# Windowed attention of layer 2: the values' shift folded into the output's, values and keys evicted by ScalarE, the output's shift added on GpSimd

## The chip, the core and the metric

The kernel is one program on one core of a Trainium2 chip. A core has five engines that run their own instruction queues side by side: TensorE (PE, with its weight loads shown as PEld), VectorE (DVE), ScalarE (ACT), GpSimd (POOL) and SyncE (SP, which here only issues transfers). The metric is the device time of one execution in microseconds; the median of five runs counts.

## What is computed

The network has four layers. Layers 0 and 1 are attentions over all tokens of a small image; layer 2 is an attention within windows of 64 tokens and then a mixture of experts; layer 3 is an additive attention and another mixture of experts. The change touches the windowed attention alone. Cut to what matters, it is:

```python
t = _to_tokens(x)                            # 2 images x 1024 tokens, 256 channels
# t = t + attention(_ln_t(t)):
x = jnp.roll(x, -shift, axis=1)              # windows shifted by half a window
qkv = xw @ w_qkv.T + b_qkv                   # 8 heads of 32
sim = jnp.einsum('bwphd,bwqhd->bhwpq', q, k) * scale + rel_pos[:, idx]
probs = jax.nn.softmax(sim, axis=-1)
out = jnp.einsum('bhwpq,bwqhd->bwphd', probs, v)
out = out @ w_out.T + b_out
```

The tokens `t` then go through a layer norm, a router and the experts.

## The kernel before

The 2048 tokens are 16 tiles (NT) of 128 tokens, 8 tiles (IT) for each image; a tile holds two windows of 64. All tokens stay in SBUF in one tensor `t`. `window_attention` first loads its weights and shifts, norms the first image and turns it to channels by partitions (`normed(0)`). Then it runs a loop of 20 slots, in which the steps of several tiles overlap:

- `value(i)`: the values of tile i, two matmuls into PSUM (`ps_va`), taken to SBUF (`va`) by VectorE, which adds the row `b_v` on the way (line 893 of the profile).
- `scores(i)`: 32 small matmuls (`ps_s`), then on VectorE scale and bias (`l`, L868), maximum (`wa_m`, L874), subtraction (L875); the exponential on ScalarE (L876); the sum (L877) and its inverse (`wa_rec`, L878) on VectorE; and on GpSimd the product with the inverse into one of three `probs` buffers (L881, two instructions).
- `turn(i - 2)`: eight transposes of `probs` on TensorE (`ps_pt`, L900), two evictions by ScalarE (`ptT`, L901).
- `project(g, part)`: while tiles are left, one quarter of the next group's queries (`qh`, evicted by ScalarE, L850) or keys (`kh`, evicted by VectorE, L852). A group is four tiles.
- `sums(i - 3)`: 16 small matmuls (`ps_av`), evicted by ScalarE (`oT`, L917).
- `output(i - 4)`: two matmuls (`ps_wo`), then VectorE adds the row `b_out` (`y`, L927) and GpSimd adds `y` to the tile of `t` (L928).

In the first six slots the loop also draws on `normed(1)`, the norm and the transposes of the second image (`ps_tr`, L832, evicted at L834). From slot 10 on it draws three steps a slot from `late.dispatch(2, 0)`, which routes the first image for the experts: the statistics of the tiles that are ready (`n_st`, L1079, which reads `t`), an inverse root (`ir_...`, L1064 to L1071), the normed tokens (`u`, L1089), their transposes (L1100), the router (L1129), the slots' numbers (`rt_...`), and 16 indirect transfers from GpSimd's queue that scatter the tokens to memory (`slots_in`, L1153). The experts read them back (`xr`, L1363), and their weights are fetched on GpSimd's queue too (`ew`, L1314).

All PSUM tiles of the loop but `ps_s` and `ps_av` come from one pool of three buffers (`late.misc`), so each new one waits until the third before it is evicted. The order of the instructions on TensorE and ScalarE is the program's (`tc.manual_schedule(engines={engines.PE, engines.Activation})`). On VectorE, GpSimd and SyncE a scheduler orders them by its own estimate of when each is ready. The order on every engine is fixed before the program runs, and each engine works strictly in it.

Of the kernel before, what the change touches and what calls it, by code (L numbers as in the profile page):

```python
# [19 lines left out]
F32 = mybir.dt.float32  # L20
I32 = mybir.dt.int32
U32 = mybir.dt.uint32
AF = mybir.ActivationFunctionType
ALU = mybir.AluOpType
# [3 lines left out]
P = 128  # L28
B, C, N = 2, 256, 1024
T = B * N  # L30
NT = T // P
CC = C // P
# [32 lines left out]
def broadcast(ap, shape):  # L65

    return ap.unsqueeze(len(shape) - 1).to_broadcast(shape)


class Stack:  # L70
# [699 lines left out]
    def window_attention(self, t, late):  # L770
# [5 lines left out]
        tc, nc = self.tc, self.nc  # L776
        H, D = 8, 32
        with ExitStack() as ctx:
            w = ctx.enter_context(tc.tile_pool(name="wa_w", bufs=1))
            sb = ctx.enter_context(tc.tile_pool(name="wa_sb", bufs=2))  # L780
# [4 lines left out]
            w_qkv = self.load(w, "w_qkv", "(c p) o -> p c o", p=P)  # L785
            w_out = self.load(w, "wa_w_out", "(c p) o -> p c o", p=P)
            b_qk = self.load(w, "b_qk")
            b_v, b_out = self.load_row(w, "b_v"), self.load_row(w, "wa_b_out")


            rel = self.ins["rel_pos"]
# [1 line left out]
            bias = w.tile([P, H, WIN], F32, name="bias")  # L793
# [18 lines left out]
                nc.gpsimd.memset(x, 0.0)  # L812

            uT, q, k, v, pT, o = {}, {}, {}, {}, {}, {}

            def normed(b):

                u = w.tile([P, IT, C], F32, name="u")
                uT[b] = w.tile([P, CC, N], F32, name=f"uT{b}")
                mv = self.mv[:, b * IT : (b + 1) * IT, :]  # L820
                rs = late.inverse_root(mv[:, :, 1], 1e-5)
                yield
                for i in range(IT):
                    nc.vector.tensor_scalar(
                        u[:, i, :], t[:, b * IT + i, :], mv[:, i, 0:1], rs[:, i : i + 1], ALU.subtract, ALU.mult
                    )
                yield
                for half in range(2):
                    for c in range(CC):
                        ps = late.misc([P, 4, P], "ps_tr")  # L830
                        for j in range(4):
                            nc.tensor.transpose(ps[:, j, :], u[:, 4 * half + j, c * P : (c + 1) * P], self.ident)  # L832
                        to = uT[b][:, c, half * CH : (half + 1) * CH].rearrange("p (k t) -> p k t", t=P)
                        (nc.scalar.copy if c else nc.vector.tensor_copy)(to, ps)  # L834
                        yield

            def project(g, part):

                if part == 0:
                    q[g], k[g] = (sb.tile([P, CC, CH], F32, name=n) for n in ("qh", "kh"))  # L840
                x, at = uT[g // 2], g % 2 * CH
                ps = late.misc([P, CH], "ps_qk")
                for c in range(CC):
                    nc.tensor.matmul(  # L844
                        ps, lhsT=w_qkv[:, c, part * P : (part + 1) * P], rhs=x[:, c, at : at + CH],
                        start=(c == 0), stop=(c == CC - 1),
                    )
                to = (q if part < CC else k)[g][:, part % CC, :]
                if part < CC:
                    nc.scalar.activation(to, ps, AF.Identity, bias=b_qk[:, part : part + 1])  # L850
                else:
                    nc.vector.tensor_scalar(to, ps, b_qk[:, part : part + 1], None, ALU.add)  # L852

            def scores(i):

                g, at = i // 4, (i % 4) * P
                s = p_s.tile([P, 4, CH], F32, name="ps_s")
                for o in range(CC):
                    for h in range(4):
                        rows = slice(D * h, D * (h + 1))  # L860
                        for r in range(2):
                            cols = slice(at + WIN * r, at + WIN * (r + 1))
                            nc.tensor.matmul(
                                s[WIN * r : WIN * (r + 1), h, WIN * o : WIN * (o + 1)],
                                lhsT=q[g][rows, o, cols], rhs=k[g][rows, o, cols], start=True, stop=True,
                            )
                l = sb.tile([P, H, WIN], F32, name="l", bufs=3)
                nc.vector.scalar_tensor_tensor(  # L868
                    l.rearrange("p (h o) k -> p h (o k)", o=CC), s[:, :, : CC * WIN], float(D) ** -0.5,
                    (last if (i + 1) % IT == 0 else bias).rearrange("p (h o) k -> p h (o k)", o=CC),  # L870
                    ALU.mult, ALU.add,
                )
                m, rec = (self.small.tile([P, H], F32, name=f"wa_{n}") for n in ("m", "rec"))
                nc.vector.tensor_reduce(m, l, AX.X, ALU.max)  # L874
                nc.vector.tensor_tensor(l, l, broadcast(m, [P, H, WIN]), ALU.subtract)  # L875
                nc.scalar.activation(l, l, AF.Exp)  # L876
                nc.vector.tensor_reduce(m, l, AX.X, ALU.add)  # L877
                nc.vector.reciprocal(rec, m)  # L878
                for r in range(2):
                    rows = slice(WIN * r, WIN * (r + 1))  # L880
                    nc.gpsimd.tensor_tensor(  # L881
                        probs[i % RING][rows, :, rows], l[rows], broadcast(rec[rows], [WIN, H, WIN]), ALU.mult
                    )

            def value(i):
                x = uT[i // IT][:, :, i % IT * P : (i % IT + 1) * P]
                v[i] = sb.tile([P, C], F32, name="va", bufs=4)
                ps = late.misc([P, C], "ps_va")
                for c in range(CC):
                    nc.tensor.matmul(  # L890
                        ps, lhsT=x[:, c, :], rhs=w_qkv[:, c, 2 * C :], start=(c == 0), stop=(c == CC - 1)
                    )
                nc.vector.tensor_tensor(v[i], ps, b_v, ALU.add)

            def turn(i):
                pT[i] = sb.tile([P, H, P], F32, name="ptT")
                for half in range(2):
                    ps = late.misc([P, H // 2, P], "ps_pt")
                    for h in range(H // 2):
                        nc.tensor.transpose(ps[:, h, :], probs[i % RING][:, H // 2 * half + h, :], self.ident)  # L900
                    nc.scalar.copy(pT[i][:, H // 2 * half : H // 2 * (half + 1)], ps)  # L901

            def sums(i):

                ps, x, y = p_av.tile([P, CC, P], F32, name="ps_av"), pT.pop(i), v.pop(i)
                for o in range(CC):
                    for h in range(4):
                        at = D * (4 * o + h)
                        nc.tensor.matmul(
                            ps[D * h : D * (h + 1), o, :], lhsT=y[:, at : at + D], rhs=x[:, CC * h + o, :],  # L910
                            start=True, stop=True,
                        )
                to_o(i, ps)
# [5 lines left out]
            def output(i):  # L919
                x = o.pop(i)  # L920
                ps = late.misc([P, C], "ps_wo")
                for c in range(CC):
                    nc.tensor.matmul(
                        ps, lhsT=x[:, c, :], rhs=w_out[:, c, :], start=(c == 0), stop=(c == CC - 1)
                    )
                y = sb.tile([P, C], F32, name="y")
                nc.vector.tensor_tensor(y, ps, b_out, ALU.add)  # L927
                nc.gpsimd.tensor_tensor(t[:, i, :], t[:, i, :], y, ALU.add)  # L928

            for _ in normed(0):  # L930
                pass
# [2 lines left out]
            with tc.manual_schedule(engines={engines.PE, engines.Activation}):  # L934
                for part in range(2 * CC):
                    project(0, part)
                for i in range(NT + 4):
                    if i < NT:
                        value(i)
                        scores(i)  # L940
                    if 2 <= i < NT + 2:
                        turn(i - 2)
                    if i + 4 < NT:
                        project(i // 4 + 1, i % 4)
                    if i < 6:
                        next(other, None)
                    if 3 <= i < NT + 3:
                        sums(i - 3)
                    if 4 <= i:
                        output(i - 4)  # L950
                    if i >= 10:
                        for _ in range(3):
                            next(route, None)
# [875 lines left out]
```

## Time and profile before

| | us |
|---|---|
| median of 5 runs | 2952.39 (2951.13 to 2954.48) |
| the profiled execution | 2956.82 |
| its span | 2955.1 |
| busy in the span: PE / DVE / ACT / POOL | 2719.4 / 1949.4 / 1828.7 / 1240.5 |
| the windowed attention: first norm to last scatter | about 1689 to 1868 |
| mean granted TensorE clock | 0.962 |

Times in the trace are counted from the span's start. The rows of a timeline are start, length, engine, line, operation, what is written and read, and in brackets how long the engine had been idle and who ended that. A row of the chain of waits is start, length and what held the end up at that moment. In a table by windows each engine's entry is its busy time and, in brackets, its instructions.

### The profile page before, as it was taken

To read this page: it belongs to the slowest core of one execution; us is meant where nothing else is said; L and a number is where in the kernel's file an instruction comes from. 1 tells how busy PE (TensorE), PEld (TensorE's weight loads), DVE (VectorE), ACT (ScalarE), POOL (GpSimd) and SP (SyncE) were. 2 spreads that over 40 slices of the span, in tenths; PEclk is the share of its full clock that TensorE was granted. 3 is DMA by queue.
4 is the path that set the end of the run, shared out by engine and by line. 5 is a ranking of instruction groups with operands and counts; after the bars stand their busy time and mean duration, and the time that the engine had idled before them with its cause. 6 is when DMAs were issued, how large, how long until landed. Compare 5 with 4: busy or idle time off the path is not lost. (4 is left out here: it accounts for less than half of the span.)

```text
span 2955.1 us, 77089 instructions
## 1 busy us (share of the span) xinstructions
PE 2719.4 (92%) x32006; PEld 1678.7 (57%) x32006; DVE 1949.4 (66%) x3642; ACT 1828.7 (62%) x2685; POOL 1240.5 (42%) x1302
## 2 busy tenths in 40 slices
PE   7899999999999999789999787899899989899987
PEld 3455555555555555555555445799666633355676
DVE  5899999999999999568778667543522343124242
ACT  2777777777777777345555322111499889788722
POOL 4777777777777777201111132443211021102142
PEclk9999999999999999899999897899999989899998
DMA  3000000000000000111110000443222010322354
GB/s 130 2 3 3 3 3 3 3 3 3 3 3 3 3 3 3 36 32 24 24 24 17 10 19 3 152 164 101 83 79 76 24 31 20 136 67 84 112 162 126
DMA packets 180574, 131.37 MB, mean 44 GB/s; under 512 B 130992, under 2 KB 162368, under 8 KB 173056
## 3 DMA queue, kind: packets, MB, share of 16 engines
q0 software_dynamic: 29232, 81.71, 8.3%
q1 hardware_dynamic: 149552, 44.27, 6.7%
q8 instruction: 251, 4.11, 0.6%
q10 hardware_dynamic: 1440, 0.47, 0.1%
q14 instruction: 99, 0.81, 0.1%
HBM read 181.24 MB, written 29.49 MB: 71 GB/s over the span
## 5 line engine op out<-in xcount | busy, mean ns | idle before, releaser
L143 PE MATMUL ps_s<-kT,qT 64*32 64x512 f32 x8192 | 605.9, 598 | 15.0 <-ACT sc L153 14.4
L200 DVE STREAM_TRANSPOSE wt<-sc 128x1024 f32<-128x1024 f32 x512 | 602.2, 1210 | 2.5 <-ACT sc L188 2.5
L188 ACT ACTIVATE sc<-sc,sa_shift 128x1024 f32<-128x1024 f32 x512 | 584.2, 1145 | 9.8 <-DMA sa_shift<-sa_min 9.5
L1614 ACT ACTIVATE th<-kT,qb 128x1024 f32<-128x1024 f32 x512 | 540.3, 1134 | 69.3 <-PE ps_e L1623 44.6
L210 PEld LDWEIGHTS ps_o<-wt,v 128*64 128x64 f32 x8192 | 446.4, 138 | 214.8 <-issue 206.8
L210 PE MATMUL ps_o<-wt,v 128*64 128x128 f32 x8192 | 506.3, 277 | 7.6 <-DVE oT L367 7.6
L153 ACT COPY sc<-ps_s 128x1024 f32<-128x1024 f32 x256 | 259.1, 1012 | 293.1 <-DVE sa_min L178 154.9
L166 POOL TENSOR_TENSOR fold<-sc 128x512 f32<-128x512 f32 x256 | 330.1, 1289 | 256.1 <-ACT sc L153 256.1
L168 POOL TENSOR_TENSOR fold<-sc,fold 128x512 f32<-128x512 f32 x256 | 328.1, 1282 | 21.4
L1623 PE MATMUL ps_e<-th,pick 128*32 128x512 f32 x2048 | 306.8, 620 | 22.1 <-ACT th L1614 9.5
L143 PEld LDWEIGHTS ps_s<-kT,qT 64*32 64x32 f32 x8192 | 166.4, 106 | 271.4 <-issue 156.7
L1396 PEld LDWEIGHTS ps_h<-xe,ew 128*128 128x128 f32 x2320 | 277.2, 194 | 62.9 <-issue 38.2
L150 DVE TENSOR_SCALAR_CACHE_REDUCE sc<-ps_s 128x1024 f32<-128x1024 f32 x256 | 303.9, 1187 | 8.2 <-PE ps_s L143 8.2
L1396 PE MATMUL ps_h<-xe,ew 128*128 128x128 f32 x2320 | 294.4, 280 | 12.5 <-DVE xe L1379 7.0
L1416 PE MATMUL ps_y<-ew,h 128*128 128x256 f32 x1160 | 276.4, 388 | 8.3 <-ACT h L1402 5.7
L1416 PEld LDWEIGHTS ps_y<-ew,h 128*128 128x128 f32 x1160 | 215.9, 193 | 66.9 <-issue 23.0
L622 ACT ACTIVATE sc<-sc,l_least 128x1024 f32<-128x1024 f32 x128 | 146.7, 1147 | 126.6 <-DVE sc L609 126.3
L1407 DVE TENSOR_TENSOR hb<-ps_h,ew 128x512 f32<-128x512 f32 x115 | 79.4, 691 | 206.5 <-PE ps_h L1396 164.8
L1420 DVE COPY y<-ps_y 128x256 f32<-128x256 f32 x99 | 42.0, 424 | 231.8 <-PE ps_y L1416 211.4
L1385 ACT ACTIVATE h<-hb 128x512 f32<-128x512 f32 x115 | 71.5, 623 | 192.3 <-DVE hb L1407 160.0
L628 DVE STREAM_TRANSPOSE wt<-sc 128x1024 f32<-128x1024 f32 x128 | 153.3, 1225 | 46.4 <-ACT sc L622 25.7
L609 DVE TENSOR_SCALAR_CACHE_REDUCE sc<-ps_s 128x1024 f32<-128x1024 f32 x128 | 150.6, 1212 | 39.3 <-PE ps_s L601 39.1
(286 smaller groups left out, 3149.2 us busy)
## 6 DMA issues: line engine op xcount, KB each, us to landing
xr<-slots_in SPq DMA_DIRECT2D x99, 128.0 KB
slots_out<-y SPq DMA_DIRECT2D x99, 128.0 KB
sa_got<-sa_least SPq DMA_DIRECT2D x512, 0.5 KB
sa_shift<-sa_min SPq DMA_DIRECT2D x512, 0.2 KB
slots_in<-zero POOLq DMA_DIRECT2D x46, 128.0 KB
sa_sums<-sa_total SPq DMA_DIRECT2D x256, 1.0 KB
kh<-kh SPq DMA_DIRECT2D x32, 128.0 KB
qh<-qh SPq DMA_DIRECT2D x32, 128.0 KB
```

What stands on the lines that cost most here:

```text
L143: nc.tensor.matmul(ps[r][S * c : S * (c + 1), a, :].rearrange("p (b i) -> p b i", i=S), lhsT=qT[half, p, S * i : S * (i + 1)], rhs=keys[ha ...
L150: nc.vector.tensor_scalar(scores[m][0], flat[0], 1.0, None, ALU.mult, ALU.min, accum_out=least[m // 2][:, 0, h : h + 1])
L153: nc.scalar.copy(scores[m][1], flat[1])
L166: nc.gpsimd.tensor_tensor(y, a, b, ALU.subtract)
L168: nc.gpsimd.tensor_tensor(y, a, y, ALU.subtract)
L188: nc.scalar.activation(scores[m][r], scores[m][r], AF.Exp, bias=shift[m // 2][:, r : r + 1], scale=-1.0, accum_out=total[i][:, 2 * p + r, ...
L200: nc.vector.transpose(weights[i, h][:, 2 * p + r, :], x)
L210: nc.tensor.matmul(sums[i][64 * k : 64 * (k + 1)], lhsT=v[:, at % NT, 64 * (at // NT) : 64 * (at // NT + 1)], rhs=weights[i, h][:, :, S * ...
L1396: nc.tensor.matmul(ps[:, j, :], lhsT=a[:, c, at : at + P], rhs=x[:, c, :], start=(c == 0), stop=(c == CC - 1),)
L1416: nc.tensor.matmul(ps, lhsT=h[:, j, :], rhs=w2[:, j, :], start=(j == 0), stop=(j == HB - 1))
L1614: nc.scalar.activation(h, keys, AF.Tanh, bias=self.qb[b][:, s // G, g : g + 1])
L1623: nc.tensor.matmul(pe[i][c * U : (c + 1) * U, a, :], lhsT=self.pick[:, k, :], rhs=h[:, a, :], start=(k == 0), stop=(k == G - 1),)
```

## The change

The values are no longer shifted. As each row of `probs` sums to one, the shift `b_v` passes through the weighted sum unchanged, so that `b_v @ w_out` can be added once to `b_out` (`output_shift`: GpSimd spreads `b_v` over 128 columns, four passes of TensorE multiply it by `w_out`, VectorE adds the result to `b_out`). `b_v` is loaded as two columns by SyncE's queue instead of as a row by ScalarE's. The values are then only copied, by ScalarE, and the keys are evicted by ScalarE like the queries. GpSimd adds `b_out` to each tile of `t`, written two slots ahead of that tile's `output`, and VectorE adds the product `ps_wo` to `t` directly; `y` is gone.

```diff
-            b_v, b_out = self.load_row(w, "b_v"), self.load_row(w, "wa_b_out")
+            b_v, b_out = self.load(w, "b_v", "(c p) -> p c", p=P), self.load_row(w, "wa_b_out")
...
+            spread = w.tile([P, CC, P], F32, name="spread")
+            nc.gpsimd.tensor_copy(spread, broadcast(b_v, [P, CC, P]))
+
+            def output_shift():
+                ps = late.misc([P, C], "ps_wo")
+                for c in range(CC):
+                    nc.tensor.matmul(
+                        ps, lhsT=spread[:, c, :], rhs=w_out[:, c, :], start=(c == 0), stop=(c == CC - 1)
+                    )
+                nc.vector.tensor_tensor(b_out, b_out, ps, ALU.add)
...
                 to = (q if part < CC else k)[g][:, part % CC, :]
-                if part < CC:
-                    nc.scalar.activation(to, ps, AF.Identity, bias=b_qk[:, part : part + 1])
-                else:
-                    nc.vector.tensor_scalar(to, ps, b_qk[:, part : part + 1], None, ALU.add)
+                nc.scalar.activation(to, ps, AF.Identity, bias=b_qk[:, part : part + 1])
...
-                nc.vector.tensor_tensor(v[i], ps, b_v, ALU.add)
+                nc.scalar.copy(v[i], ps)
...
-                y = sb.tile([P, C], F32, name="y")
-                nc.vector.tensor_tensor(y, ps, b_out, ALU.add)
-                nc.gpsimd.tensor_tensor(t[:, i, :], t[:, i, :], y, ALU.add)
+                nc.vector.tensor_tensor(t[:, i, :], t[:, i, :], ps, ALU.add)
...
                 for part in range(2 * CC):
                     project(0, part)
+                output_shift()
                 for i in range(NT + 4):
...
+                    if 2 <= i < NT + 2:
+                        nc.gpsimd.tensor_tensor(t[:, i - 2, :], t[:, i - 2, :], b_out, ALU.add)
                     if 3 <= i < NT + 3:
                         sums(i - 3)
```

## The prediction

> **What bounds the kernel now.** I first read the table by windows for the stage that the change touches, then the chain of waits through it, the waits, the groups, and last the timeline at its two ends. 0.2% of the time, 5.9 us, is about what a measurement of this kernel can tell from no change.
>
> ```profile
> 1713.00:1728.00 15.00, 12.09 (x150) 6.66 (x156) 13.02 (x22) 4.01 (x7) 4.16 (x4) 1.00 0.01 2
> 1728.00:1750.00 22.00, 18.91 (x248) 12.15 (x244) 12.92 (x25) 8.03 (x16) 9.78 (x10) 1.00 0.01 1
> 1800.00:1845.00 45.00, 30.80 (x283) 22.40 (x281) 37.70 (x136) 9.14 (x21) 11.47 (x13) 0.74 0.00 1
> 1845.00:1875.00 30.00, 15.57 (x76) 9.68 (x76) 13.61 (x58) 1.55 (x4) 23.92 (x26) 0.65 0.37 130
> ```
>
> The columns are PE, PEld, DVE, ACT, POOL, then the granted clock. No engine is full throughout: DVE holds the first slots (13.0 of 15.0) and the routing (37.7 of 45.0), POOL the tail (23.9 of 30.0). In between a slot is a loop over four engines, which the chain of waits shows:
>
> ```profile
> 1753.34 0.70 DVE wa_m L877
> 1754.43 1.04 POOL probs L881
> 1755.55 1.05 POOL probs L881
> 1756.67 0.74 POOL t L928
> 1757.43 0.44 DVE n_st L1079
> 1758.07 0.59 DVE l L868
> ```
>
> The next tile's scores (L868) stand on DVE behind the statistics of `t` (L1079), and these wait for POOL's addition (L928), itself queued behind `probs`. In the waits of the stage (total, times, longest) and its groups:
>
> ```profile
> DVE n_st L1079 <- POOL t L928: 10.7, 7, 3.4
> POOL probs L881 <- DVE wa_rec L878: 41.7, 6, 27.0
> ```
>
> ```profile
> L881 POOL TENSOR_TENSOR probs<-l,wa_rec 64x512 f32<-64x512 f32 x32 | 33.3, 1041 | 76.7 <-DVE wa_rec L878 41.7 <-ACT ptT L901 22.7 <-ACT oT L917 5.3
> L928 POOL TENSOR_TENSOR t<-t,y 128x256 f32<-128x256 f32 x16 | 11.7, 732 | 34.2 <-DVE y L927 14.3 <-DVE rt_ends L1249 9.0 <-DVE ir_a L1069 6.9
> L893 DVE TENSOR_TENSOR va<-ps_va,sb_b_v 128x256 f32<-128x256 f32 x16 | 6.6, 416 | 6.5 <-PE ps_va L890 6.3
> ```
>
> After the attention 1080 us of experts and layer 3 follow, reached only through the scatter; I carry what the stage gains or loses to the end.
>
> **Part 1, the start (a loss).** In the changed kernel as built, POOL's queue does not hold the sixteen additions of `b_out` two slots ahead: all sixteen stand in a row behind the spreading copy and before the first `probs`. The scheduler orders POOL, and once `b_out` is known nothing holds an addition back. In the trace of before:
>
> ```profile
> 1718.05 2.16 POOL L881 TENSOR_TENSOR probs<-l,wa_rec 64x512 f32<-64x512 f32 x2 [26.99 <-DVE wa_rec L878]
> ...
> 1719.18 1.57 DVE L875 TENSOR_TENSOR l<-l,wa_m 128x512 f32<-128x512 f32 x1
> ...
> 1720.26 0.66 PE L900 MATMUL ps_pt<-ident,probs 128*128 128x128 f32 x4
> ...
> 1728.52 0.69 DVE L868 SCALAR_TENSOR_TENSOR l<-ps_s,bias 128x512 f32<-128x512 f32 x1
> ```
>
> The queries and keys end on PE at 1712.5. Then come the four passes of `output_shift` (like `ps_va` x4, 0.86) to 1713.4 and DVE's addition (0.42, as L927) to 1713.9. POOL's sixteen additions take 0.71 each (1.42 for two in a row, L928 at 1860.08), 11.4 in all, to 1725.4; if the subtractions (L875) of tiles 0 to 2 each push one back by 0.69, to 1727.5. I take 1726.3. The first `probs` (2.16) then ends at 1728.5 instead of 1720.2, and TensorE stands at `turn(0)` for 8 us, with `project`, `value(3)` and `scores(3)` queued behind it and ScalarE's `ptT` waiting too. From `turn(0)` to L868 of tile 3 PE then has 0.93 + 1.9 + 0.66 + 0.96 + 0.5 = 5.0 us of work by warm rows (`ps_pt`, `ps_qk`, `ps_tr`, `ps_va`, `ps_s`). After the idle time before 1703.4 the granted clock was 0.50 up to 1707 and a pass of `ps_qk` took 1.19 instead of 0.59, so I add about 1.1, between 0 (warm) and 2 (cold all through). L868 comes at 1734.6 instead of 1728.52: **+6.1**, between +4.1 (1725.4, warm) and +8.5 (1727.5, cold).
>
> In the row at 1719.18 DVE's subtraction took 1.57, elsewhere 0.69: it waited for POOL's second `probs` to end. The Trainium skill, in SBUF — State Buffer, Who interferes with whom, says of a VectorE instruction with two SBUF inputs and a GpSimd instruction that reads SBUF that whichever issues second is blocked until the first has finished. By it alone all three subtractions would hold POOL's row up, and the start would cost 1.2 us more than I take (a row's end at 1727.5); the row shows only DVE's side. It is the rule that speaks against moving additions to POOL here.
>
> The new spreading copy (POOL idle for 27 us before 1718, by the waits) and the two-column load (issued at about 1700 where `turned`, its neighbour on SP, landed by 1705.8) have 6 us until 1712.5: nothing. `turned` moves by one issue, 0.46, and is needed at 1713.9. If that cover failed, the load would add its lateness one for one, by 1 us at most as `turned`'s time suggests.
>
> **Part 2, tiles 4 to 15 (a gain).** POOL's addition leaves the loop, and DVE adds `ps_wo` to `t` at the cost of `y` (0.42). `va` (16 of 0.42) and `kh` (8 of 0.75) leave DVE. What is late next is mostly PE's `ps_s`. For each tile I compare the start of L868 with the end of its `ps_s`, less 0.1, or with the DVE work left. Tiles 5 and 6: `ps_s` ends at 1741.9, L868 starts at 1742.7, and the same again: 0.7 each. Tile 7: `ps_s` ends at 1756.25, L868 starts at 1758.0: 1.6. Tiles 8, 9, 10, 11: 0.5, 1.1, 1.3, 1.1 (in 10 and 11 `n_st` waits 1.93 and 0.89 for POOL). Tile 12: 0.4, since the router's passes on PE end it. Tile 13 is the large one: PE waits 4.43 us for `u` (L1089), whose inverse root stands on DVE behind `n_st`, the sum and a POOL-blocked step (0.91); in the changed order the root is done beside the scores, and the four `u` follow the addition of `ps_wo` at once, at 1804.2 instead of 1806.9 to 1809.1: 3.4. Tiles 14 and 15: 0.5 each, little but the `va`. Sum **-11.8**. From above it is bounded by all that DVE loses in work and waits in the stage, 6.6 + 6.0 + 10.7 = 23; from below by tiles 7, 10, 11 and half of 13, 1.6 + 1.3 + 1.1 + 1.7 = 6.
>
> ScalarE pays 16 x 0.39 (as `oT`, L917) + 8 x 0.69 (as `qh`, L850) = 11.8 us. In a slot it stands between the second `ptT` and the next exponential: at 1754.27 and 1760.19 these leave 5.9 us, and `kh`, `oT` and `va` need 1.5. So I cost it at nothing; the cover goes if `va` ends after `scores` on PE, and then a slot pays up to 0.4. The PSUM buffer that `va` holds comes free earlier, where PE waited 0.74 for it (`ps_qk` at 1773.78).
>
> **Part 3, the tail (a gain).**
>
> ```profile
> 1848.88 0.97 POOL L1153 DMA_INDIRECT slots_in<-u,rt_slot  x1 [0.30 <-issue]
> 1849.91 0.72 POOL L928 TENSOR_TENSOR t<-t,y 128x256 f32<-128x256 f32 x1
> 1850.78 0.99 POOL L1153 DMA_INDIRECT slots_in<-u,rt_slot  x1 [0.15 <-issue]
> ```
>
> The 16 scatters run 1.28 us apart; where an addition stands between them, 1.90, 1.89 and (two) 2.56. In the changed order none does: 0.62 + 0.61 + 1.28 = **-2.5**. The experts' first fetches stand behind the scatters on the same queue and move with them. Off the end's path, DVE no longer waits 4.65 for POOL at 1856.
>
> **Sum.** 6.1 - 11.8 - 2.5 = -8.2 us. It is made on the execution of 2956.82, 4.4 above the median; as a difference it goes to the median: 2952.4 - 8.2 = **2944.2**. Its own range: from 4.1 - 16 - 3 = -15 to 8.5 - 6 - 2 = +0.5.
>
> **Rivals.**
>
> *The gain is eaten by the next engine (no change).* If ScalarE's extra copies lengthen its part of the loop by 0.4 in twelve slots, 4.8 of Part 2 is gone, and the sum is -3.4: 2949.0. For it: every slot passes through `l`, `ptT` and PE. Against it: the 5.9 us of room.
>
> *The row of additions (slower).* One mechanism: sixteen additions at the length of the `probs` instructions (1.04), because DVE holds POOL up all the way, take 16.6 and end at 1730.5. That is 4.2 later than I took, with a cold clock +1 more: the start costs 11.3. With Part 2 at its lower bound of 6 and Part 3 at 2 the kernel is 3.3 slower, 2955.7. It decides once the start costs more than the other two bring; 5.9 us slower needs a start of 14 us or hardly any gain. For it: a start whose whole stall falls on TensorE. Against it: L928 takes 0.73 wherever it stands.
>
> *The additions do not run as a row* (one of them waits for something that comes slot by slot): the start costs 1 and the sum is -13.3: 2939.1. Against it: the instruction order and the absence of a later producer.
>
> **How the numbers follow.** The forecast gets 0.55, the early-finishing version 0.07, the eaten gain 0.23, the slower one 0.15. Faster by over 5.9 us: most of the forecast (0.50) and all of the 0.07, so 0.57. Slower by over 5.9: the upper part of the slower rival, 0.10. Within: the rest, 0.33. The range that leaves out 2 in 10 goes from 2937 (most of Part 2's upper bound) to 2956 (the slower rival's middle).
>
> **What would show it.** Right: on POOL one unbroken row of additions from about 1714 to 1726; `turn(0)` at about 1728.6 with the clock at 0.5 after it; no wait of `n_st` for POOL; L868 6 late at tile 3, some 2.5 late at tile 8, level at tile 10 and some 5 ahead at tile 13; 16 scatters at 1.28 with nothing between, ending 8 us earlier. Wrong: a first `probs` near 1720; waits of TensorE for `va` or `kh` on ScalarE; an end of the scatters near 1868 or later; or a length from the first expert to the end other than 1080 us by more than 2, which nothing in my steps provides for.

## Result and profile after

| | before | after |
|---|---|---|
| median of the timed runs | 2952.89 us (44 runs) | 2952.09 us (24 runs) |
| ratio after / before, 95% interval | | 0.9996 (0.9991 to 1.0002) |
| profiled execution | 2956.82 us | 2943.32 us |

The change gains nothing that this measurement can show: 0.8 us, between a gain of 2.7 and a loss of 0.6. The profiled execution after lies below all 24 timed ones (the lowest is 2948.42), so its total is not compared, only its stages. They are counted from the first `ps_qk` (1703.42 before, 1698.65 after; the difference comes from the load of `w_qkv`, which the change does not touch). Lines of the changed kernel are about ten higher: L877 is the old L868 (`l`), L884 the old L875 (the subtraction), L890 `probs`, L1163 the scatters, L1191 the addition of the experts' bias, L1373 `xr`, L1381 `ps_x`.

The start, in the timeline:

```profile
1709.37 12.33 POOL L956 TENSOR_TENSOR t<-t,sb_wa_b_out 128x256 f32<-128x256 f32 x16 [8.54 <-DVE sb_wa_b_out L826]
1711.68 1.02 DVE L884 TENSOR_TENSOR l<-l,wa_m 128x512 f32<-128x512 f32 x1
1721.66 6.57 POOL L890 TENSOR_TENSOR probs<-l,wa_rec 64x512 f32<-64x512 f32 x6
1723.87 1.97 PE L909 MATMUL ps_pt<-ident,probs 128*128 128x128 f32 x8 [7.37 <-POOL probs L890]
1730.11 0.69 DVE L877 SCALAR_TENSOR_TENSOR l<-ps_s,bias 128x512 f32<-128x512 f32 x1 [0.75 <-PE ps_s L872]
```

The unbroken row is there: sixteen additions in 12.33 us, behind them `probs` of three tiles at once, and TensorE waits 7.37 for the first. The groups of the stage show the rest of the exchange:

```profile
L890 POOL TENSOR_TENSOR probs<-l,wa_rec 64x512 f32<-64x512 f32 x32 | 33.7, 1052 | 74.7 <-ACT ptT L910 37.0 <-DVE rt_one L1266 9.8 <-DVE n_mv L1090 9.1
L956 POOL TENSOR_TENSOR t<-t,sb_wa_b_out 128x256 f32<-128x256 f32 x16 | 12.3, 809 | 8.5 <-DVE sb_wa_b_out L826 8.5
L902 ACT COPY va<-ps_va 128x256 f32<-128x256 f32 x16 | 5.9, 372 | 26.3 <-PE ps_va L899 26.3
```

`va` costs ScalarE 5.9 us and nobody waits for it, and the waits of `n_st` for GpSimd are gone from the waits of the stage. `l` (L877) of the tiles, and the steps behind them, in us after the first `ps_qk`:

| | tile 3 | tile 8 | tile 13 | tile 15 | last scatter ends | `xr` issued | first `ps_x` |
|---|---|---|---|---|---|---|---|
| before | 25.10 | 62.27 | 113.78 | 134.29 | 164.33 | 165.90 | 170.90 |
| after | 31.45 | 65.18 | 105.26 | 124.75 | 152.00 | 154.54 | 168.13 |
| difference | +6.35 | +2.91 | -8.52 | -9.54 | **-12.33** | -11.36 | **-2.77** |

So in these two profiles the stage gains 12.3 us up to the last scatter, more than I forecast (e4 below shows that 2.2 of them go with a lower clock in the one profile before), and 9.6 are gone when the first expert's transposes (`ps_x`) run. The window of the tail (columns as above) and the timeline say where:

```profile
1840.23:1870.23 30.00, 12.97 (x40) 9.13 (x41) 11.54 (x45) 0.00 (x0) 14.01 (x15) 0.50 0.68 266
```

```profile
1847.00 3.78 PE L1189 MATMUL ps_b<-sb_l_b,wT 8*128 8x256 f32 x8 [3.64 <-issue]
1849.68 0.97 POOL L1163 DMA_INDIRECT slots_in<-u,rt_slot  x1 [0.31 <-issue]
1850.96 1.06 POOL L1324 DMA_INDIRECT ew<-in_l_up,rt_rows  x1 [0.30 <-issue]
1853.19 14.63 SPq L1373 DMA_DIRECT2D xr<-slots_in  x4
1855.36 0.69 DVE L1191 TENSOR_TENSOR t<-t,ps_b 128x512 f32<-128x512 f32 x1 [7.11 <-remote]
1861.74 0.69 DVE L1191 TENSOR_TENSOR t<-t,ps_b 128x512 f32<-128x512 f32 x1 [5.42 <-remote]
1863.07 3.78 PE L1189 MATMUL ps_b<-sb_l_b,wT 8*128 8x256 f32 x8 [5.95 <-DVE wT L1183]
1866.78 0.69 PE L1381 MATMUL ps_x<-ident,xr 128*128 128x128 f32 x2
```

On TensorE's queue the transposes and passes of the experts' bias (`ps_wT`, `ps_b`, the end of `dispatch(2, 0)`) stand ahead of the first `ps_x`. VectorE's additions of it waited 7.11 and 5.42 us with a releaser that the trace calls "remote": the semaphore that they wait for was updated just before they began, but no instruction that updates it had just ended. It is TensorE's own semaphore, and by the profile, which models the ends of matmuls, the passes `ps_b` that these additions need had all ended by 1850.8. `ps_x` came straight behind the second tile group's `ps_b`, without a wait of its own; the packets of the first `xr` moved between 1855.5 and 1857. In the kernel before the same place looks like this:

```profile
1871.12 0.90 PE L1100 MATMUL ps_tr<-ident,u 128*128 128x128 f32 x3
1871.22 0.69 DVE L1181 TENSOR_TENSOR t<-t,ps_b 128x512 f32<-128x512 f32 x1 [0.69 <-PE ps_b L1179]
1874.32 0.66 PE L1371 MATMUL ps_x<-ident,xr 128*128 128x128 f32 x2 [2.30 <-DMA xr<-slots_in]
```

The bias was done 3.1 us earlier, and `ps_x` waited for `xr`, that is for the scatters.

Behind `ps_x` TensorE has no gap for 175 us in either kernel. From `ps_x` to the end it took 1080.8 before and 1074.6 after; remote waits lie in that stretch as well.

### The profile page after: what moved, and what is told of

The parts are those of the page before. It is cut to its first block, busy times and chain, and to the rows that moved or that the text cites. A ratio compares the mean times of both kernels' runs of the same rounds, so it can differ in the third digit from the quotient of the medians.

```text
span 2941.4 us, 77095 instructions
## 1 busy us (share of the span) xinstructions
PE 2704.8 (92%) x32010; PEld 1672.4 (57%) x32010; DVE 1935.2 (66%) x3619; ACT 1839.6 (63%) x2709; POOL 1240.2 (42%) x1303
```

## Experiments

The runs fall into two conditions, and no number here can be read without that: in some sessions every profile has remote waits, in others none has one.

| session | kernel before, median | remote waits in the profiles |
|---|---|---|
| first comparison (above) | 2952.89 | 68.4 (before), 70.5 (after) |
| e1 to e4 | 2913.56 | none |
| e5 to e8 | 2948.26 | 46.9 to 67.2 |
| e9 to e11 | 2912.73 | none |
| e12 | 2953.72 | 92.7 |

All ratios are to the kernel before in the same session. The kernel before itself has no profile without remote waits; e4, which only moves the experts' bias behind the first experts, is nearest to one.

**e1, the changed kernel again** (no edit).

> The changed kernel once more, for its stage lengths. Theory Q (TensorE's queue): the stage's gain reaches the last scatter (12 us earlier, counted from the first ps_qk) and is lost before the first expert: the first ps_x stands on TensorE behind the passes ps_b of the experts' bias, and the additions of these on VectorE (L1191) wait several us. It expects the waits of L1191 again (12 us in sum; 3 at the least), ps_x only 1 to 5 us earlier than in the kernel before counted from the first ps_qk, and a time within 3 us of the kernel before. Rival O (a one-off): the two waits belong to that one execution. It expects L1191 without waits over 1 us, ps_x 10 us earlier, and a total that is still within 3 us because the gain goes later. Rival D (transfers): ps_x comes when xr and the weights have landed, whatever TensorE's queue holds; L1191 may wait or not.

Measured: ratio 0.9956 (0.9943 to 0.9969), 2900.51 against 2913.56: **a gain of 13.0 us** (9 to 17 by the interval). The last scatter ends at 152.31 and `ps_x` comes at 158.93, that is 12.0 before the place that it had in the kernel before, and 9.8 before its place in e4. In the timeline:

```profile
1849.00 0.69 DVE L1191 TENSOR_TENSOR t<-t,ps_b 128x512 f32<-128x512 f32 x1 [0.95 <-PE ps_b L1189]
1856.75 5.93 SPq L1373 DMA_DIRECT2D xr<-slots_in  x4
1861.67 0.66 PE L1381 MATMUL ps_x<-ident,xr 128*128 128x128 f32 x2 [12.70 <-DMA xr<-slots_in]
```

The bias is done 12 us before `ps_x`, and `ps_x` waits for `xr`. Q and O had expected a time within 3 us of the kernel before, and missed. Without the waits the path is the one of the prediction, through the scatter.

**e2, the additions kept out of the row.** The order of GpSimd is written by hand for slots 0 to 9, and eight of these slots add to two tiles each.

```
-            with tc.manual_schedule(engines={engines.PE, engines.Activation}):
+            with tc.manual_schedule(engines={engines.PE, engines.Activation, engines.Pool}):
...
-                    if 2 <= i < NT + 2:
-                        nc.gpsimd.tensor_tensor(t[:, i - 2, :], t[:, i - 2, :], b_out, ALU.add)
+                if 2 <= i < 10:
+                    for n in (i - 2, i + 6):
+                        nc.gpsimd.tensor_tensor(t[:, n, :], t[:, n, :], b_out, ALU.add)
```

> The sixteen additions of b_out are kept out of the row: GpSimd's order is written by hand for slots 0 to 9, and slots 2 to 9 each add to two tiles behind probs. The start's loss of 6.1 should go: probs of tile 0 within 1.5 us of wa_rec, L877 of tile 3 at +0.5 instead of +6.4 against the kernel before (from the first ps_qk). Price: 1.5 us of GpSimd in eight slots, which has 3.9 of 6 us free in a slot: 0 to 2 us in all. The last scatter then ends 4 to 6 us earlier than in the changed kernel. Theory Q: what the scatter gains is carried only as far as ps_x, so that total and change differ by -5 (if the waits of VectorE move with the stage) to 0 (if they grow by as much). Rival D: 4 to 6 us less in total.

Measured: ratio 0.9940 (0.9927 to 0.9954), 4.35 us less than e1. The two intervals overlap, but five of e2's six executions are faster than all six of e1.

```profile
1728.59 0.69 DVE L877 SCALAR_TENSOR_TENSOR l<-ps_s,bias 128x512 f32<-128x512 f32 x1 [1.10 <-PE ps_s L872]
1728.88 1.40 POOL L953 TENSOR_TENSOR t<-t,sb_wa_b_out 128x256 f32<-128x256 f32 x2
```

Tile 3 starts at 26.70 (e1: 31.77), 5.1 earlier and 1.6 later than in the kernel before, where I had expected 0.5; the scatters end 3.3 and `ps_x` comes 3.5 earlier. So the row costs 5.1 at the start; 1.8 of what is won there is lost again by tile 15, and the rest reaches the end. The 4 to 6 expected at the scatter was a little too much.

**e3 and e4, the experts' bias behind the first experts**, in the changed kernel and in the kernel before.

```
-        if l == 2:
+        if key == (2, 1):
             yield from self.shift(*key)
...
+            "B20": (self.shift(2, 0), ("D20",), 60, 6.0),
-            "C20": (self.collect(2, 0), ("E20",), 172, 2.0),
+            "C20": (self.collect(2, 0), ("E20", "B20"), 172, 2.0),
```

> The changed kernel, with the experts' bias of the first group (transposes ps_wT, passes ps_b, additions to t) taken out of the route and emitted as a step of its own 60 us into the experts; on TensorE the first ps_x now follows the last ps_wo and the router's passes of the next group. Theory Q: ps_x comes 4 to 7 us after the issue of xr (it was 13.6), 8 to 10 us earlier than in the changed kernel, and from there TensorE is busy without a gap, so the total falls by 7 to 10 us: 2942 to 2945. Rival D: ps_x or the first ps_h wait for xr or for the weights instead, and the total is that of the changed kernel within 2 us. Rival O: as D, since the loss lies later.

> The kernel before with the same move of the experts' bias. There ps_x was ended by xr itself (2.30 us of waiting for that transfer, 5.0 us after its issue), so theory Q expects at most 1 us of gain: 2951 to 2953; with the run before it, the change itself is then worth 7 to 10 us. Rival D: the same for both kernels, 0. If the bias's work costs time wherever it stands in the experts, this kernel gains 3 us or more as well and the difference between the two stays near 1.

Measured: e3 0.9964 (0.9951 to 0.9976), 2.9 us slower than e1, with overlapping intervals; e4 1.0017 (1.0006 to 1.0027), slower than the kernel before.

```profile
1860.81 0.66 PE L1381 MATMUL ps_x<-ident,xr 128*128 128x128 f32 x2 [12.16 <-DMA xr<-slots_in]
```

In e3 `ps_x` comes at 159.00, as in e1: with no waits on VectorE there is nothing to free, and the bias's work, which lay in TensorE's idle time before `ps_x`, now stands in a stretch without gaps. Theory Q's gain did not come, and D was right for this condition. Between e4 and e3 the scatters end 9.7 earlier (162.09 to 152.44), and so does `ps_x` (168.73 to 159.00): carried one for one. The medians of the two differ by more, 15.3.

e4 leaves the windowed attention as it was and so shows one thing more of it. Tile 12's `ps_va` in the kernel before and in e4:

```profile
1796.73 2.05 PE L890 MATMUL ps_va<-sb_w_qkv,uT 128*128 128x256 f32 x4
1794.46 1.11 PE L890 MATMUL ps_va<-sb_w_qkv,uT 128*128 128x256 f32 x4
```

The granted clock was 0.51 from 1796 to 1803 in the kernel before, and 1.00 at the same place of e4 (1794 to 1801); tiles 12 to 14 took 3.2 us longer there than in e4, and the scatters ended 2.2 later after the first `ps_qk`. Whether other executions of the kernel before have this dip is not shown.

**e5, the changed kernel a third time** (no edit).

> The changed kernel a third time, as the reference of the three runs beside it, and to tell two theories of the lost gain apart. Theory C (the chip): the waits that the trace marks as remote (70.5 us of them in the first execution of the changed kernel, 68.4 in that of the kernel before, none in the four runs since) belong to the chip that it ran on. Expected: either a kernel before near 2913 us, no such waits and a gain of 12 to 14 us, or one near 2952, such waits of 60 to 80 us and a gain under 3 us. Theory O (one execution): the waits come and go on the same chip; expected then a kernel before near 2913 with some of them, or one near 2952 without.

Measured: ratio 0.999 (0.998 to 1.0), kernel before 2948.26. The waits are back, at the same place:

```profile
1853.56 0.69 DVE L1191 TENSOR_TENSOR t<-t,ps_b 128x512 f32<-128x512 f32 x1 [6.70 <-remote]
1861.29 0.68 DVE L1183 COPY wT<-ps_wT 8x512 f32<-8x512 f32 x1 [7.04 <-remote]
1865.73 0.69 PE L1381 MATMUL ps_x<-ident,xr 128*128 128x128 f32 x2
```

The scatters end at 151.92 as always, and `ps_x` comes at 165.77. The waits are no accident of one execution (O falls); they come and go by session, and with them some 35 to 41 us of the time of the kernel before. Theory C holds as far as that, with a correction from e12.

**e6 and e7, the two halves.** e6 keeps the copies on ScalarE and the folded shift, but gives the output back to VectorE and GpSimd:

```
-                nc.vector.tensor_tensor(t[:, i, :], t[:, i, :], ps, ALU.add)
+                y = sb.tile([P, C], F32, name="y")
+                nc.vector.tensor_tensor(y, ps, b_out, ALU.add)
+                nc.gpsimd.tensor_tensor(t[:, i, :], t[:, i, :], y, ALU.add)
...
-                    if 2 <= i < NT + 2:
-                        nc.gpsimd.tensor_tensor(t[:, i - 2, :], t[:, i - 2, :], b_out, ALU.add)
```

e7 keeps the new output, but copies values and keys on VectorE:

```
-                nc.scalar.copy(v[i], ps)
+                nc.vector.tensor_copy(v[i], ps)
...
-                nc.scalar.activation(to, ps, AF.Identity, bias=b_qk[:, part : part + 1])
+                if part < CC:
+                    nc.scalar.activation(to, ps, AF.Identity, bias=b_qk[:, part : part + 1])
+                else:
+                    nc.vector.tensor_scalar(to, ps, b_qk[:, part : part + 1], None, ALU.add)
```

> One half of the change alone: values and keys on ScalarE with the values' shift in the output's, but the output as in the kernel before (VectorE makes y from ps_wo and b_out, GpSimd adds y to t in the slot). My steps: no row of additions, so the start costs 1 (four passes of output_shift), the slots gain what VectorE loses of va and kh where it was late (tiles 5, 6, 8, 9, 11 to 15: 4 to 6), the waits of n_st for GpSimd stay, the tail gains nothing: -3 to -5 against the kernel before. If ScalarE's longer part of the slot eats the gain (the rival of the prediction), 0 to +3.

> The other half alone: the changed kernel, but with values and keys copied on VectorE as before (copy 0.42, keys 0.75 each). The row of additions stands: +6. The slots gain the waits for GpSimd (tiles 7, 10, 11: 4) and tile 13 (3.4 by the prediction, 5.6 by the trace), the tail 2.5: -4 to -6 in sum against the kernel before. With the other half's -3 to -5 that does not reach the -13 of the whole unless the halves help each other; a sum within 2 us of the whole says that they are independent.

| against the kernel before | at tile 3 | end of scatters | from tile 3 on | `ps_x` | ratio |
|---|---|---|---|---|---|
| e6, ScalarE's half | +1.63 | -1.79 | -3.42 | -1.53 | 0.9981 (0.9970 to 0.9992) |
| e7, the output's half | +7.39 | -7.24 | -14.63 | -5.61 | 0.9991 (0.9981 to 1.0000) |
| whole change | +6.35 | -12.33 | -18.68 | -2.77 | 0.9996 (0.9991 to 1.0002) |

From tile 3 on the halves add up (18.05 of 18.68) against this one profile of the kernel before; against e4 they are 1.1 and 12.3 of 16.4, so that adding up is not shown to better than 3 us. In a sum of the first two columns the start, which both pay, is counted twice. Most of the gain is the output's either way. I had expected more of e6's half at the scatter (3 to 5) and less of e7's (4 to 6). e6 has no remote wait between the first scatter and `ps_x`; e7 has two long ones on VectorE (7.01 and 4.78) and loses 1.6 of its gain to them.

**e8, additions in the slots and `output_shift` in slot 1.**

```
                 for part in range(2 * CC):
                     project(0, part)
-                output_shift()
...
+                if i == 1:
+                    output_shift()
                 if 2 <= i < NT + 2:
                     turn(i - 2)
```

> The additions in slots 2 to 9 (as in the second run, 4.4 us faster than the changed kernel), and output_shift moved from ahead of slot 0 into slot 1, behind the scores of tile 1, so that tile 0's scores do not wait for its four passes. L877 of tiles 0 to 2 should start 0.9 to 1.2 earlier, tile 3 as the kernel before (25.1 after the first ps_qk, it was 26.7). In the total -0.5 to -1.5 against the second run if the start is carried to the end, 0 if tile 3 to 5 wait for another engine: 2912 - 17 to -19 on a chip like that of the last runs.

Measured: tile 3 at 25.60, scatters' end at 148.27, 0.8 before e2's. Ratio 0.9973 (0.9960 to 0.9985) in a session with remote waits, where VectorE's 6.76 and 7.02 before `ps_x` put that at 163.58.

**e9, e11 and e12, the row of scatters broken.** GpSimd copies a piece of `u` onto itself behind the 8th and the 12th scatter; e9 is the changed kernel with it, e11 and e12 are e8 with it.

```
                 before.append(ins)
+            if key == (2, 0) and i in (3, 5):
+                x = u[:, i - 2 : i + 2 : 3, 0:P]
+                nc.gpsimd.tensor_copy(x, x)
             yield None if l == 2 else 0.5
```

> The changed kernel with its row of 16 scatters and 6 weight fetches broken twice: GpSimd copies a piece of u onto itself (128x2x128) behind the 8th and the 12th scatter, as the additions to t stood between the scatters of the kernel before. Nothing is left out. Theory R (the row): on a chip with remote waits, VectorE's long ones beside the scatters (12.5 us at L1191 and L1183 in the first execution, 13.7 in the third run) come from the unbroken row of indirect transfers, and go when it is broken: no remote wait over 3 us on VectorE between the first scatter and ps_x; the last scatter ends 1 to 4 us later, ps_x comes 4 to 6 us after the issue of xr (11.5 and 13.6 before), and the total falls by 4 to 8 us against the changed kernel, to a ratio near 0.997 of the kernel before. Rival P (the place in the program, or the load of the transfers): the waits stay as they are, and the total is 1 to 3 us longer than the changed kernel. On a chip without remote waits both expect +1 to +3 against the changed kernel.

> The fastest form so far (additions in slots 2 to 9, output_shift in slot 1; ratio 0.9973 on a chip with remote waits) with the row of scatters broken as in the run beside it. Theory R: on a chip with remote waits ps_x 155 to 158 us after the first ps_qk instead of 163.6, total 5 to 8 us less, ratio near 0.995. Rival P: ratio 0.9975 to 0.998. On a chip without remote waits: 1 to 3 us more than the same kernel without the breaks, some 16 us less than the kernel before.

> The same kernel once more (additions in slots 2 to 9, output_shift in slot 1, the row of scatters broken twice), to be set beside the eighth run, which is it without the breaks. Only a chip with remote waits tells the theories apart. Theory R (the unbroken row on GpSmd's queue brings VectorE's waits): no remote wait over 3 us on VectorE between the first scatter and ps_x, ps_x 155 to 158 us after the first ps_qk (163.6 in the eighth run), 4 to 6 us after the issue of xr, ratio 0.994 to 0.996. Rival P (the place in the program, or the load of the transfers): waits of 6 to 7 us at L1191 and L1183 as in the eighth run, ps_x at 162 to 166, ratio 0.997 to 0.9985. On a chip without remote waits both expect the ratio of the run before, 0.994.

Measured: e9 0.9960 (0.9947 to 0.9973) and e11 0.9942 (0.9928 to 0.9956), both in a session without remote waits: with the breaks the scatters end 1.2 later (e9 against e1), which decides nothing. e12 fell in a session with waits: 0.9983 (0.9973 to 0.9993).

```profile
1840.92 0.42 DVE L935 TENSOR_TENSOR t<-t,ps_wo 128x256 f32<-128x256 f32 x1 [5.06 <-remote]
1862.20 0.69 DVE L1202 TENSOR_TENSOR t<-t,ps_b 128x512 f32<-128x512 f32 x1 [8.85 <-remote]
1867.24 0.69 PE L1392 MATMUL ps_x<-ident,xr 128*128 128x128 f32 x2
```

The row was broken (copies at 1840.98 and 1846.34), and the waits stayed: 5.06 and 8.85 on VectorE, `ps_x` at 164.39. Theory R, that breaking the row ends the waits, falls for two such breaks. That the row has no part in them is not shown: these breaks make it only 0.6 us longer than in e8, the additions in the kernel before make it 2.6 longer. The two profiles with additions between the scatters, the kernel before and e6, have no remote wait from the bias's first step to `ps_x`, and the other five with remote waits all have some there. The session also corrects theory C: its chip bears the same number as that of e1 to e4, which had no such waits. So the condition belongs to the session and is not shown to be a property of a chip.

**e10, the bias later, again.**

> The changed kernel with the experts' bias moved behind the first experts, again, for a chip with remote waits. Theory R: VectorE's waits are tied to the row on GpSimd and not to the bias, so whatever VectorE takes from TensorE there (the router's transposes of the next group, which now stand ahead of ps_x) is held up as well: remote waits of 5 us and more remain between the scatters and ps_x, and ps_x gains less than 5 us on the changed kernel. Theory Q in its narrow form (only the bias's additions are caught): ps_x 4 to 7 us after the issue of xr and no long wait ahead of it. On either kind of chip the passes of the bias then cost 3 to 6 us later, inside the stretch in which TensorE has no gap, as the third run showed (1044.7 from ps_x to the end, 1036.0 without the move).

Measured: 0.9977 (0.9967 to 0.9987), in a session without remote waits, where it only repeats e3: `ps_x` at 159.24, 5 us slower than e9 beside it, with overlapping intervals. Whether the move helps where the waits are was not measured.

## Why the prediction was right and where it failed

The time lay in the range (2937 to 2956), by the wrong way: the forecast was a gain of 8.2, and measured was 0.8.

- **Part 1, the start: right.** Forecast +6.1 at tile 3, measured +6.35; the row lasted 12.33 where I took 12.4, 0.77 an addition on average. That is not the 1.04 of the slower rival. VectorE's three subtractions beside it took 1.02, 0.95 and 0.93 instead of 0.69, and each time the next addition took 1.17 or 1.18 instead of 0.72: the subtraction waited for the addition under way, and the next addition for the subtraction. That is the pattern of the Trainium skill's rule (SBUF — State Buffer, Who interferes with whom). It cost the row some 0.46 us a time, and not the 0.69 with which I had put the rule's end of the row at 1727.5, a row of 13.6. e2 is the rival without a row, made on purpose: 5.1 less at the start, 4.35 in the total, where the forecasts differed by 5.1.
- **Part 2, the slots: mechanism right, one term too small.** Forecast -11.8 from tile 4 to tile 15, measured -15.9, just inside the 16 that my range took, but only -12.9 between e4 and e1. Seven of the steps (tiles 5 to 8, 11, 14, 15) are within 0.1. Too small were tiles 9, 10 and 12 by 0.5 to 0.8 and above all tile 13: 3.4 against 5.55 (4.3 between e4 and e1, where tile 12 gains nothing). I had moved `u` to 1804.2 and left the router's and TensorE's passes behind it as they were; the whole chain of the inverse root moved. Tiles 12 to 14 of the one trace before, on which I built, also ran 3.2 us longer than in e4 at a lower clock; that stands in my rows as in the difference measured against them.
- **ScalarE at no cost: right.** e6's half gains 3.4 from tile 3 on (1.1 against e4). The rival of the eaten gain named ScalarE, and ScalarE was not it.
- **Part 3, the tail: right.** Forecast -2.5, measured -2.79 from tile 15 to the end of the scatters (-3.5 between e4 and e1).
- **The sum failed at its last step**, "reached only through the scatter; I carry what the stage gains or loses to the end". The first expert needs `xr`, but on TensorE also all that is queued ahead of `ps_x`: `ps_wT` and `ps_b` with VectorE's steps between them. In the trace before this second path ended 3.1 us ahead of `ps_x`, and behind three transposes `ps_tr` TensorE stood ready 2.3 ahead of it. I read the wait that came last (2.30 for `xr`) and did not see that it is also the distance of the next path. With the scatters 12.3 earlier, this path had to come as much earlier too, less 3.1. By its work it does, as e1 shows. In sessions with remote waits it is held up by 12 to 14 us and ends last. "A length other than 1080 from the first expert to the end" stood in my list of what would prove the prediction wrong; it was 1074.6 and 1071.9 with remote waits, and 1036 without.
- **Not knowable from one profile**: that there is a second condition. The waits of the kernel before listed 68.4 us of remote waits, none of them between the bias and `ps_x`. They were a sign that any chain of small steps between TensorE and VectorE in this part might be held up, and I priced none.

What is shown: the stage's gain at the scatter (9.7 to 12.3 us), that it reaches the end without remote waits (e1: 13.0 us), and that with them VectorE's waits in the bias's path take most of it (`ps_x` -2.8 and -5.1 in two executions). Both executions were faster than the median of the timed ones, so where those lose the rest is not shown.

The traces tell more of the remote waits than their name. They fall on instructions that wait for TensorE (`ps_b`, `ps_wT` and `ps_wo` for VectorE, `ps_av` for ScalarE), while short steps that wait for VectorE itself run between them. All 125 of them that last over 0.5 us, in seven profiles, ended with an update of TensorE's semaphore. In the seven profiles without such waits this update follows the modelled end of TensorE's last instruction that makes it by 0.02 us in the median, and only the last two of the kernel come more than 0.3 us behind it. In the seven with them 37 to 53 updates come over 1 us behind it, all of these after the first scatter, and the semaphores of VectorE and ScalarE are not late. So the name misleads: TensorE finished late, or its update came late. A fall of the clock did not start them: in the profiles after and e5 it was still 1.00 during the first of these waits, and fell to 0.50 behind it.

Not shown is which of the two it is, and why. The Trainium skill (Perfetto Trace Analysis, Per-engine timelines) says that a semaphore's way to the other engines lies outside the recorded window. That allows for a late update; as the ends of matmuls are modelled, a late end would look the same. Two breaks in the row of indirect transfers did not remove the waits; the load of the transfers and the place in the program remain untried.

The fastest form was that of e2 and e11, 0.9940 and 0.9942 without remote waits; with them the same idea, e8, reached 0.9973 and e12 0.9983.

## What to carry to other kernels

Before a gain is carried through a transfer, ask of the consumer's engine what else is queued ahead of it, and by how much that path ended earlier: that slack (here 2.3 to 3.1 us) is all that is safe. An operation "two slots ahead" stands where the scheduler puts it: without a producer that arrives slot by slot, sixteen additions became a row that cost 5 us; an order written by hand gave them back. Where a profile lists waits that no finished instruction explains, look up whose semaphore ended them, and measure the change in more than one session before believing either answer. And a single profile of the kernel before carries its own clock into the difference, here 3.2 us in three tiles.

## What was not expected of the hardware

The same kernel before took about 2913 us in two sessions and 2948 to 2954 in three, and the difference came with 47 to 93 us of remote waits in the profiles against none, all of them for TensorE's semaphore and all behind the first scatter; `ps_x` to the end was 1036 us in e1 and 1072 in e5, the same program. What comes before did not differ: the first `ps_qk` came at 1702.74 in e1 and 1699.96 in e5, and tile 15 started 124.98 and 124.72 after it.
